# Self attention of a Perceiver layer: the value product and its way back move into the loop, the Ev product is turned in 32x32 blocks by VectorE, each batch enters the next stage by itself, two PSUM banks are kept across stages

## The chip, the cores and the metric

The kernel runs on one core of a Trainium2 chip, all in fp32. The metric is device time in microseconds (us). The core has five engines, each with a queue of its own that is worked off in order: TensorE (PE in the profile, its weight loads PEld), VectorE (DVE), ScalarE (ACT), GpSimd (POOL) and SyncE (SP), which here only starts transfers. TensorE writes to PSUM, eight banks of 128 partitions by 512 floats; the other engines bring results from there to SBUF. Engines wait for one another by semaphores.

## The reference

The shapes are x (4, 128, 512), ctx (4, 2048, 512), 16 heads of 32.

```python
x = x + xattn(layernorm(x), ctx, ctx)   # softmax over heads and batch (axis 0)
x = x + attn(layernorm(x))
x = x + ffn(layernorm(x))               # an attention too, with gates

def attn(x):        # rel[l,m] = clip(l - m, -64, 64) + 64
    q, k, v = heads(x @ Wq), heads(x @ Wk), heads(x @ Wv)
    logits = (q k^T + q . Ek[rel] + k . Eq[rel] + Eq[rel] . Ek[rel]) / sqrt(32)
    p = softmax(logits)                  # over m
    return p @ v + einsum('bhlm,lmd->bhld', p, Ev[rel])
```

The last term is the Ev product: for each row l there is another table Ev[rel[l, :]] of 128 by 32, common to the 64 pairs of head and batch.

## The kernel before, in words

Three stages follow each other: cross attention to about 661 us, self attention to 789.7, the gated attention ("ffn") to the end. The order of instructions in each engine's queue is the order in which the code issues them (`manual_schedule`); semaphores are put in between by the framework, for each use of a tile and for the reuse of a buffer. A pool with `bufs=n` holds n buffers, given out in turn; a new tile waits for the last reader of the one that it takes the place of.

Layouts: `x1` is [position, batch, 512]. `xT`, `qT`, `kT` and `oT` have features on the partitions: four chunks c of 128 features, four heads i in each, and columns (batch, position). `lg` and `eT` hold 64 tiles of 128x128, one for each f = (c, i, batch), in `lg` with rows l, in `eT` with rows m. "Group c" below means the four heads of chunk c, 16 tiles.

*The head of stage 2.* `layernorm_T` (L151) of stage 1 leaves x1 and xT, and at its end copies x out of PSUM (L224). `queries` and `keys` project; `spread` (L614) sorts q and k by position into `z`; `relative_k` and `relative_q` multiply them with the windows of Ek and Eq and lay the results into `rk` and `lg`. `ev_win`, the windows of Ev, then takes the place of `z`. PSUM: three banks `ps`, one `psz` (both opened for stage 2), and two pairs `ps4`, which `banks` takes together.

*The loop.* `logits(c)` transposes 16 tiles of rk into four banks (L717) and adds q k^T on top (L730). `join(c)` (L746, VectorE) adds the four banks to `lg`, `largest(c, i)` (L752, VectorE) takes the negated maximum, `exponentials_of(c, i)` (L757, ScalarE) are four instructions with a sum each, `softmax(c, i)` is a reciprocal on VectorE (L763) and a product on GpSimd (L764), `transposed(c, i)` four transposes (L772) and a copy to `eT` (L773; VectorE for heads 0 and 1, ScalarE for 2 and 3). A round issues `logits(c+1)`, all 16 exponentials of group c, all of join(c+1), and then, head by head, `largest(c+1, i)`, `softmax(c, i)` and `transposed(c-1, i)`:

```python
for c in range(C):
    if c + 1 < C:
        ps = logits(c + 1)
    for i in range(NH):
        exponentials_of(c, i)
    if c + 1 < C:
        join(c + 1, ps)
    for i in range(NH):
        if c + 1 < C:
            largest(c + 1, i)
        softmax(c, i)
        if c:
            transposed(c - 1, i)
```

*The end of stage 2.* Behind the loop, `attend(c)` puts the transposed x1 into a bank (L783), adds the products of v and eT for 16 pairs of head and batch (L795), and the sum goes to `oT` (L803). The Ev product (L848) multiplies, for each position p = 32 g + j, the window of Ev (128x32) with the 64 columns of `eT` at p; row group g of a bank gets the result. Each of four banks holds eight j. From there 32 VectorE adds (L863, 32 partitions each) and 32 ScalarE copies (L865) with two GpSimd adds (L869) bring it into `oT`; 16 transposes (L873) turn `oT` back to rows of x, in four banks. `layernorm_T` takes statistics of each batch there, normalises, transposes (L232) to xT, with `idle` matmuls (L149) between, and copies the banks to x1 (L224).

*Stage 3* opens with eight other banks, four `psl` and four `ps`. Five bias rows are loaded by GpSimd's queue (L897 to L901). For each batch `queries(b)` (L244, with an add on VectorE and a square on ScalarE), `lengths` and `normalised` follow; then keys, transposed queries, its own loop over groups, gates, and the output product. The weights of stage 3 are loaded by SP's queue (L47), each as soon as the buffer is free.

Of the kernel before, what the change touches and what calls it, by code (L numbers as in the profile page):

```python
# [16 lines left out]
def perceiver_layer(ctx: ExitStack, tc: tile.TileContext, a: dict, out: bass.AP):  # L17
# [32 lines left out]
    def load_const(name, shape, src, pool=const):  # L50
        t = pool.tile(shape, F32, tag=name, name=name)
        nc.gpsimd.dma_start(out=t, in_=src)
        return t

    def load_row(name, n, pool=const):
        return load_const(f"row_{name}", [P, n], a[name].partition_broadcast(P), pool)
# [195 lines left out]

    with s1:
# [5 lines left out]
        ps_g = s1.enter_context(tc.tile_pool(name="s1_ps", bufs=2, space=PSUM))  # L259
# [4 lines left out]

        def bank(n):
            return ps_g.tile([P, 512], F32, tag="ps", name=f"ps_{n}")
# [86 lines left out]
        def exponentials_of(n, c):  # L353
            nc.scalar.activation(sg[n, c], sg[n, c], AF.Exp, scale=SCALE)  # L354
# [229 lines left out]
    with ExitStack() as s2:  # L584
# [4 lines left out]
        ps1 = s2.enter_context(tc.tile_pool(name="s2_ps", bufs=3, space=PSUM))  # L589
        psz = s2.enter_context(tc.tile_pool(name="s2_psz", bufs=1, space=PSUM))  # L590
        ps4 = s2_loop.enter_context(tc.tile_pool(name="s2_ps4", bufs=2, space=PSUM))

        def bank(n):
            return ps1.tile([P, 512], F32, tag="ps", name=f"s2_{n}")

        def bank_z(n):
            return psz.tile([P, 512], F32, tag="psz", name=f"s2_{n}")
# [64 lines left out]
        def values(b, between=None):  # L662

            ps = bank(f"v{b}")
            for k in range(C):
                if between and k == C // 2:
                    between()
                nc.tensor.matmul(  # L668
                    ps, lhsT=xT[:, k, b * T : (b + 1) * T], rhs=awv[:, k, :], start=(k == 0), stop=(k == C - 1)
                )  # L670
            nc.scalar.copy(v[:, b, :], ps)

        def queries(c):
            ps = bank(f"q{c}") if c < 3 else bank_z("q3")
            project_T(ps, awq, xT, c)
            (nc.scalar.mul if c % 2 else nc.vector.tensor_scalar_mul)(qT[:, c, :], ps, SCALE)

        def keys(c):
            ps = bank(f"k{c}") if c < 3 else bank_z("k3")
            project_T(ps, awk, xT, c)  # L680
            (nc.scalar.copy if c % 2 else nc.vector.tensor_copy)(kT[:, c, :], ps)
# [61 lines left out]
        def join(c, ps):  # L743
            for i in range(NH):
                fs = of_head(c, i)
                nc.vector.tensor_tensor(  # L746
                    lg[:, fs, :], ps[i].rearrange("p (b m) -> p b m", b=B), lg[:, fs, :], ALU.add
                )
# [12 lines left out]
        def softmax(c, i):  # L761
            fs = of_head(c, i)
            nc.vector.reciprocal(rs[:, fs], rs[:, fs])  # L763
            nc.gpsimd.tensor_tensor(  # L764
                lg[:, fs, :], lg[:, fs, :], rs[:, fs].unsqueeze(2).to_broadcast([P, B, T]), ALU.mult
            )

        def transposed(c, i):
            ps = bank(f"t{c}_{i}")
            fs = of_head(c, i)  # L770
            for b in range(B):
                nc.tensor.transpose(ps[:, b * T : (b + 1) * T], lg[:, fs.start + b, :], ident)  # L772
            (nc.scalar.copy if i >= 2 else nc.vector.tensor_copy)(  # L773
                eT[:, fs, :], ps.rearrange("p (b l) -> p b l", b=B)
            )


        oT = one.tile([P, C, B, T], F32, tag="qT", name="oT2")

        def attend(c, eng):  # L780
            ps = bank_z(f"o{c}") if c % 2 else bank(f"o{c}")
            for b in range(B):
                nc.tensor.matmul(  # L783
                    ps[:, b * T : (b + 1) * T],
                    lhsT=x1[:, b, c * P : (c + 1) * P],
                    rhs=ident,
                    is_transpose=True,
                    start=(b == 0),
                    stop=False,
                    skip_group_check=True,  # L790
                )
            for b in range(B):
                for i in range(NH):
                    h = c * NH + i
                    nc.tensor.matmul(  # L795
                        ps[i * HD : (i + 1) * HD, b * T : (b + 1) * T],
                        lhsT=v[:, b, h * HD : (h + 1) * HD],
                        rhs=eT[:, h * B + b, :],
                        start=False,
                        stop=True,  # L800
                        skip_group_check=True,
                    )
            eng(oT[:, c].rearrange("p b l -> p (b l)"), ps)  # L803

        ps = logits(0)
        join(0, ps)
        for i in range(NH):
            largest(0, i)
        for c in range(C):
            if c + 1 < C:  # L810
                ps = logits(c + 1)
            for i in range(NH):
                exponentials_of(c, i)
            if c + 1 < C:
                join(c + 1, ps)
            for i in range(NH):
                if c + 1 < C:
                    largest(c + 1, i)
                softmax(c, i)
                if c:  # L820
                    transposed(c - 1, i)
        s2_loop.close()
        psq = s2.enter_context(tc.tile_pool(name="s2_psq", bufs=4, space=PSUM))

        def bank_q(n):
            return psq.tile([P, 512], F32, tag="psq", name=f"s2_{n}")


        nc.scalar.activation(small.tile([P, 1], F32, tag="rt", name="rt2"), eps, AF.Sqrt)
        attend(0, nc.vector.tensor_copy)  # L830
        attend(1, nc.vector.tensor_copy)
        for i in range(NH):
            transposed(C - 1, i)
            if i == 1:
                attend(2, nc.vector.tensor_copy)
# [4 lines left out]
        oev = one.tile([P, C * B, NG4, J8], F32, tag="kT", name="oev")  # L840
        by_8 = oT.rearrange("p c b (g n j) -> p (c b) g n j", g=NG4, j=J8)
        for n in range(NJ // J8):
            bk8 = bank_q(f"ev{n}")
            ps = bk8.rearrange("p (j f) -> p j f", f=NF)
            for j in range(J8):
                for g in range(NG4):
                    p = NJ * g + n * J8 + j
                    nc.tensor.matmul(  # L848
                        ps[g * HD : (g + 1) * HD, j, :],
                        lhsT=ev_win[:, T - 1 - p, :],  # L850
                        rhs=eT[:, :, p],
                        start=True,
                        stop=True,
                    )
            if n == 0:
                attend(C - 1, nc.vector.tensor_copy)
            for g in range(NG4):
                from_ = ps[g * HD : (g + 1) * HD].rearrange("p j (c i b) -> p i c b j", i=NH, b=B)
                for i in range(NH):
                    rows = slice(i * HD, (i + 1) * HD)  # L860
                    if n % 2:
                        to = oT[rows, :, :, g * NJ + n * J8 : g * NJ + (n + 1) * J8]
                        nc.vector.tensor_tensor(to, from_[:, i], to, ALU.add)  # L863
                    else:
                        nc.scalar.copy(  # L865
                            oev[rows].rearrange("p (c b) g j -> p c b g j", b=B)[:, :, :, g, :], from_[:, i]
                        )
            if n % 2 == 0:
                nc.gpsimd.tensor_tensor(by_8[:, :, :, n, :], by_8[:, :, :, n, :], oev, ALU.add)  # L869
        out_ps = [bank_q(f"out{b}") for b in range(B)]  # L870
        for b in range(B):
            for c in range(C):
                nc.tensor.transpose(out_ps[b][:, c * P : (c + 1) * P], oT[:, c, b, :], ident)  # L873
        idle_ps = bank_z("idle")[:, 0:P]
        xT = layernorm_T(out_ps, ps1, 2, keep=lambda k: idle(idle_ps, k))
# [9 lines left out]
    with ExitStack() as s3:  # L885
# [11 lines left out]
        fbq_row = load_row("ffn_bq", D, one)  # L897
        qe_row = load_row("ffn_query_embedding", D, one)
        fbv_row = load_row("ffn_bv", D, one)
        fbp_row = load_row("ffn_bp", D, one)  # L900
        brs_row = load_row("ffn_brs", H + 1, one)  # L901
# [17 lines left out]
        def queries(b):  # L919
            ps = bank_l(f"q{b}")  # L920
            project(ps, fwq, xT, b)
            nc.vector.tensor_tensor(q[:, b, :], ps, fbq_row, ALU.add)
# [99 lines left out]
        sqs = {0: queries(0)}  # L1022
        for b in range(B):
            lengths(b, sqs[b])
            if b + 1 < B:
                sqs[b + 1] = queries(b + 1)
            normalised(b)
# [178 lines left out]
```

## Time and profile before

| | us |
|---|---|
| runs | 874.06, 872.05, 871.6 |
| median of the runs | 872.05 |
| profiled execution | 871.75 |
| its span, first to last instruction | 869.8 |
| stage 1, to about | 661 |
| stage 2, head, to the first exponentials' inputs | 661 to 721.65 |
| stage 2, loop, to the start of the Ev product | 721.65 to 764.86 |
| Ev product | 764.86 to 775.98 |
| way back, to the first query product of stage 3 | 775.98 to 789.72 |
| stage 3, from there | 789.72 to 869.8 |

Over the span TensorE is busy 96%, VectorE 72%, ScalarE 50%, GpSimd 50%. From 661 to 721.65 TensorE is busy for 58.68 of 60.65 us; in the loop for 29.90 of 43.21, VectorE for 28.75, ScalarE for 31.66, GpSimd for 16.27; on the way back TensorE for 8.28 of 13.74, VectorE for 10.90.

How it is read: a timeline lists an engine's work in order of time: start, length, engine and line, operation, output and inputs, tile shape, count, and in brackets the idle time before it and what ended it. Neighbours of one line come as one row with a count. A window shows the busy time of each engine in a stretch (in the order TensorE, its weight loads, VectorE, ScalarE, GpSimd), then the clock that the throttle granted TensorE, as a share of full speed. In the page's row of 40 slices the same clock stands in tenths.

### The profile page before, as it was taken

To read this page: it belongs to the slowest core of one execution; us is meant where nothing else is said; L and a number is where in the kernel's file an instruction comes from. 1 tells how busy PE (TensorE), PEld (TensorE's weight loads), DVE (VectorE), ACT (ScalarE), POOL (GpSimd) and SP (SyncE) were. 2 spreads that over 40 slices of the span, in tenths; PEclk is the share of its full clock that TensorE was granted. 3 is DMA by queue.
4 is the path that set the end of the run, shared out by engine and by line. 5 is a ranking of instruction groups with operands and counts; after the bars stand their busy time and mean duration, and the time that the engine had idled before them with its cause. 6 is when DMAs were issued, how large, how long until landed. Compare 5 with 4: busy or idle time off the path is not lost. (4 is left out here: it accounts for less than half of the span.)

```text
span 869.8 us, 16501 instructions
## 1 busy us (share of the span) xinstructions
PE 831.1 (96%) x7109; PEld 450.1 (52%) x7109; DVE 625.6 (72%) x617; ACT 438.8 (50%) x730; POOL 437.9 (50%) x295
## 2 busy tenths in 40 slices
PE   9999999999999999999999999999989996779998
PEld 5454544554544545545554544544445565566564
DVE  2049688888888888988878888888963537556563
ACT  3358446465465455455464464554403555844671
POOL 1246766666757567666566757567700022512152
PEclk9999999999999999999999999999999999789999
DMA  8140010110101001010110101001101203002101
GB/s 301 34 142 2 1 49 2 49 50 1 50 1 49 11 39 50 1 50 1 50 49 2 49 2 49 2 1 50 48 2 49 96 4 146 2 2 50 50 2 49
DMA packets 10906, 35.55 MB, mean 41 GB/s; under 512 B 977, under 2 KB 1138, under 8 KB 8786
## 3 DMA queue, kind: packets, MB, share of 16 engines
q1 hardware_dynamic: 8402, 29.43, 9.5%
q10 hardware_dynamic: 1632, 3.15, 1.0%
q0 software_dynamic: 800, 1.93, 0.9%
q8 instruction: 56, 0.92, 0.4%
q14 instruction: 16, 0.13, 0.0%
HBM read 33.45 MB, written 1.05 MB: 40 GB/s over the span
## 5 line engine op out<-in xcount | busy, mean ns | idle before, releaser
L345 DVE TENSOR_TENSOR sg<-sg,stat 128x2048 f32<-128x2048 f32 x128 | 288.2, 2281 | 1.2
L354 ACT ACTIVATE sg<-sg 128x2048 f32<-128x2048 f32 x64 | 122.4, 1912 | 244.9 <-DVE sg L345 244.9
L244 PE MATMUL ps_v<-w_xattn_Wv,ct 128*128 128x512 f32 x512 | 232.6, 598 | 3.6 <-ACT v L291 3.3
L237 PE MATMUL ps_k<-ct,w_xattn_Wk 128*128 128x512 f32 x480 | 221.9, 605 | 0.8 <-ACT pos L142 0.8
L360 POOL TENSOR_TENSOR sm<-sm,sg 128x1024 f32<-128x1024 f32 x46 | 108.6, 2360 | 145.5 <-ACT sg L354 143.3
L324 DVE TENSOR_TENSOR mx<-mx,ps_s 128x1024 f32<-128x1024 f32 x96 | 117.2, 1221 | 78.1 <-ACT sg L315 65.9
L244 PEld LDWEIGHTS ps_v<-w_xattn_Wv,ct 128*128 128x128 f32 x512 | 96.3, 191 | 130.6 <-issue 113.9
L237 PEld LDWEIGHTS ps_k<-ct,w_xattn_Wk 128*128 128x128 f32 x480 | 86.2, 189 | 94.1 <-issue 86.1
L315 ACT COPY sg<-ps_s 128x1024 f32<-128x1024 f32 x128 | 124.2, 1020 | 7.2 <-DVE mx L322 3.5
L361 POOL TENSOR_TENSOR sm<-sm,sg 128x1024 f32<-128x1024 f32 x46 | 108.8, 2366 | 3.6
L292 POOL TENSOR_TENSOR v<-v,row_xattn_bv 128x512 f32<-128x512 f32 x64 | 81.7, 1277 | 41.4 <-ACT v L291 38.0
L302 PE MATMUL ps_s<-qT,kT 32*128 32x128 f32 x2048 | 75.7, 283 | 0.1
L389 PEld LDWEIGHTS pso<-sg,v 128*32 128x32 f32 x1920 | 49.2, 110 | 47.5 <-DVE mx L324 22.0
L302 PEld LDWEIGHTS ps_s<-qT,kT 32*128 32x128 f32 x2048 | 63.3, 186 | 18.0 <-issue 17.0
L389 PE MATMUL pso<-sg,v 128*32 128x128 f32 x1920 | 65.3, 277 | 3.7 <-DVE acc L402 2.1
L358 POOL TENSOR_TENSOR sm<-sg 128x1024 f32<-128x1024 f32 x16 | 37.9, 2366 | 45.3 <-ACT sg L354 45.2
L656 POOL TENSOR_TENSOR lg<-lg,pos 128x512 f32<-128x512 f32 x6 | 7.4, 1263 | 85.9 <-ACT lg L655 85.9
L285 ACT ACTIVATE kT<-ps_k,bk 128x512 f32<-128x512 f32 x64 | 44.2, 694 | 11.9 <-PE ps_k L237 6.0
L291 ACT COPY v<-ps_v 128x512 f32<-128x512 f32 x64 | 36.4, 569 | 10.1 <-PE ps_v L244 10.1
L402 DVE TENSOR_TENSOR acc<-pso,acc 128x512 f32<-128x512 f32 x54 | 36.9, 682 | 3.9 <-PE pso L389 3.9
L322 DVE TENSOR_TENSOR mx<-sg,ps_s 128x1024 f32<-128x1024 f32 x16 | 19.5, 1220 | 27.3 <-ACT sg L315 27.3
L995 POOL TENSOR_TENSOR e<-e,rs 128x512 f32<-128x512 f32 x16 | 16.3, 1041 | 40.6 <-DVE rs L994 40.6
(213 smaller groups left out, 834.7 us busy)
## 6 DMA issues: line engine op xcount, KB each, us to landing
ct<-in_ctxT SPq DMA_DIRECT2D x15, 1024.0 KB, 4.9
ev_win<-in_tabv SPq DMA_DIRECT2D x1, 2048.0 KB, 9.3
w_xattn_Wk<-in_xattn_Wk ACTq DMA_DIRECT2D x4, 256.0 KB, 7.9
ct<-in_ctxT SPq DMA_DIRECT2D x4, 256.0 KB, 6.5
x<-in_x SPq DMA_DIRECT2D x4, 256.0 KB, 8.0
w_xattn_Wv<-in_xattn_Wv ACTq DMA_DIRECT2D x1, 1024.0 KB
w_xattn_Wq<-in_xattn_Wq SPq DMA_DIRECT2D x1, 1024.0 KB, 10.4
w_xattn_Wo<-in_xattn_Wo ACTq DMA_DIRECT2D x1, 1024.0 KB, 5.3
```

Of the source, the lines that this page charges most:

```text
L237: nc.tensor.matmul(ps, lhsT=w[:, k, c * P : (c + 1) * P], rhs=src[:, k, :], start=(k == 0), stop=(k == C - 1))
L244: nc.tensor.matmul(ps, lhsT=src[:, k, b * T : (b + 1) * T], rhs=w[:, k, :], start=(k == 0), stop=(k == C - 1))
L285: nc.scalar.activation(kT[n, c], ps, AF.Identity, bias=bk[:, c : c + 1])
L292: nc.gpsimd.tensor_tensor(v[n, b], v[n, b], bv_row, ALU.add)
L302: nc.tensor.matmul(ps[i][:, cols], lhsT=kT[n, c][rows, cols], rhs=qT[rows, c, cols], start=True, stop=True)
L315: nc.scalar.copy(sg[n, c][:, k * HALF : (k + 1) * HALF], pss[n, c][k])
L324: nc.vector.tensor_tensor(mxs[n], mxs[n], pss[n, c][k], ALU.max)
L345: nc.vector.tensor_tensor(g, g, stat[:, row, :].unsqueeze(1).to_broadcast([P, NH * B, T]), op)
L354: nc.scalar.activation(sg[n, c], sg[n, c], AF.Exp, scale=SCALE)
L360: eng.tensor_tensor(t, t, g[:, 0:HALF], ALU.add)
L361: eng.tensor_tensor(t, t, g[:, HALF:], ALU.add)
L389: nc.tensor.matmul(ps[i * HD : (i + 1) * HD, b * T : (b + 1) * T], lhsT=v[n, b][:, h * HD : (h + 1) * HD], rhs=sg[n, c][:, f * T : (f + 1) ...
```

## The change

Stage 1 and the head of stage 2 keep their work; only their banks change. Two banks, `s12_ps`, live through both stages and serve the projections, `attend` and `turned_back`; two others, `s2_pst`, serve the transposes of the loop. After the loop the Ev product has one tile of four banks, `ev`.

In the loop, the exponentials of one head at a time alternate with the rest of the round. `join(0)` alternates with `largest(0, i)`, the table of the exponential is loaded before the loop, and `logits(c+2)` is issued at the end of round c. `attend(c-1)` has no x1 in it any more; its bank goes to `oT` by ScalarE (VectorE in the last round), and `turned_back` transposes `oT` and adds it to x1 on VectorE. All copies of eT of heads 2 and 3 stand inside the next group's round, between its heads 0 and 1.

Behind the loop, the Ev product goes on in one piece, with `attend(3)` after its fourth and `turned_back(3)` after its twelfth position, and 12 idle matmuls. For each batch `turn` transposes the 32x32 blocks of `ev` into `turned` in one VectorE instruction, an add (VectorE for batch 0, GpSimd for the others) brings it into x1, and statistics and the normalised `xn` of each batch follow by themselves (ScalarE). The transposes to xT move into stage 3, each batch's between the query products. The five rows go by SP's queue. The diff, cut to its core:

```diff
+    s12 = ctx.enter_context(ExitStack())
+    ps_g = s12.enter_context(tc.tile_pool(name="s12_ps", bufs=2, space=PSUM))
...
-        ps1 = s2.enter_context(tc.tile_pool(name="s2_ps", bufs=3, space=PSUM))
-        psz = s2.enter_context(tc.tile_pool(name="s2_psz", bufs=1, space=PSUM))
+        pst = s2.enter_context(tc.tile_pool(name="s2_pst", bufs=2, space=PSUM))
...
-        def join(c, ps):
-            for i in range(NH):
+        def join(c, ps, heads=range(NH)):
+            for i in heads:
...
-        def softmax(c, i):
+        def softmax(c, i, eng=nc.gpsimd):
...
-        def transposed(c, i):
-            ps = bank(f"t{c}_{i}")
+        def transposed(c, i, eng):
+            ps = bank_t(f"t{c}_{i}")
...
-        def attend(c, eng):
-            ps = bank_z(f"o{c}") if c % 2 else bank(f"o{c}")
-            for b in range(B):
-                nc.tensor.matmul(
-                    ps[:, b * T : (b + 1) * T],
-                    lhsT=x1[:, b, c * P : (c + 1) * P],
-                    rhs=ident,
-                    is_transpose=True,
...
+        def attend(c):
+            ps = bank(f"o{c}")
...
+        def attended(c, ps, eng):
+            eng(oT[:, c].rearrange("p b l -> p (b l)"), ps)
+
+        def turned_back(c):
+            ps = bank(f"ob{c}")
+            for b in range(B):
+                nc.tensor.transpose(ps[:, b * P : (b + 1) * P], oT[:, c, b, :], ident)
+            xc = x1[:, :, c * P : (c + 1) * P]
+            nc.vector.tensor_tensor(xc, ps.rearrange("p (b d) -> p b d", b=B), xc, ALU.add)
...
+        act, dve = nc.scalar.copy, nc.vector.tensor_copy
+        nc.scalar.activation(small.tile([P, 1], F32, tag="rt", name="rt4"), eps, AF.Exp)
+        ps = logits(0)
+        for i in range(NH):
+            join(0, ps, (i,))
+            largest(0, i)
+        ps = logits(1)
+        for c in range(C):
+            last = c + 1 == C
+            eng = dve if last else act
+            exponentials_of(c, 0)
+            if not last:
+                join(c + 1, ps)
+            softmax(c, 0)
+            if c:
+                transposed(c - 1, 2, eng)
+                transposed(c - 1, 3, eng)
+            if not last:
+                largest(c + 1, 0)
+            exponentials_of(c, 1)
+            softmax(c, 1)
+            transposed(c, 0, dve)
+            if not last:
+                largest(c + 1, 1)
+            if c:
+                attended(c - 1, attend(c - 1), eng)
+            exponentials_of(c, 2)
+            softmax(c, 2)
+            if c:
+                turned_back(c - 1)
+            if not last:
+                largest(c + 1, 2)
+            transposed(c, 1, dve)
+            exponentials_of(c, 3)
+            if c + 2 < C:
+                ps = logits(c + 2)
+            if not last:
+                largest(c + 1, 3)
+                softmax(c, 3)
...
+        transposed(C - 1, 2, dve)
+        softmax(C - 1, 3, nc.vector)
+        transposed(C - 1, 3, dve)
+        ev = psq.tile([P, NJ, NF], F32, tag="ev", name="ev")
+        for j in range(NJ):
+            if j == 4:
+                attended(C - 1, attend(C - 1), act)
+            if j == 12:
+                turned_back(C - 1)
...
+        idle(bank_t("idle")[:, 0:P], 12)
...
+        def turn(b):
+            nc.vector.transpose(
+                turned[:, b, :].rearrange("p (h d) -> p h d", d=HD),
+                ev.rearrange("p j (h b) -> p b h j", b=B)[:, b],
+            )
...
+        turn(0)
+        add(0, nc.vector)
+        statistics(0)
+        turn(1)
+        add(1, nc.gpsimd)
+        normalised(0)
+        turn(2)
+        add(2, nc.gpsimd)
+        statistics(1)
+        turn(3)
+        add(3, nc.gpsimd)
+        normalised(1)
+        statistics(2)
+        normalised(2)
+        statistics(3)
+        normalised(3)
...
-        fbq_row = load_row("ffn_bq", D, one)
...
+            load_row(name, n, one, nc.sync)
...
-        sqs = {0: queries(0)}
+        def x_turned(b):
+            ps = bank_l(f"xT{b}")
+            for c in range(C):
+                nc.tensor.transpose(ps[:, c * P : (c + 1) * P], xn[b][:, c * P : (c + 1) * P], ident)
+            nc.scalar.copy(xT[:, :, b * T : (b + 1) * T], ps.rearrange("p (c t) -> p c t", c=C))
+        x_turned(0)
+        ps = queries(0)
         for b in range(B):
-            lengths(b, sqs[b])
             if b + 1 < B:
-                sqs[b + 1] = queries(b + 1)
-            normalised(b)
+                x_turned(b + 1)
+            sq = queries_out(b, ps)
+            if b:
+                normalised(b - 1)
+            lengths(b, sq)
+            if b + 1 < B:
+                ps = queries(b + 1)
+        normalised(B - 1)
```

## Prediction

> **What bounds the kernel now.** I read the page first (span and granted clock), then the timeline of each engine from 655 to 805 us, the only stretch that the change reaches, then windows of 1 us there. Stage 1 issues the same instructions in the same order in both kernels, and so does stage 3 behind its query product.
>
> ```profile
> span 869.8 us, 16501 instructions
> ...
> PEclk9999999999999999999999999999999999789999
> ```
>
> The page: the clock is below full only in slices 35 and 36, the self attention. ScalarE and VectorE there (timeline; start, length, what ended the idle time before):
>
> ```profile
> 725.10 2.48 DVE L746 TENSOR_TENSOR lg<-s_l,lg 128x512 f32<-128x512 f32 x4 [2.40 <-PE s_l L730]
> 727.50 2.45 DVE L752 TENSOR_REDUCE nm<-lg 128x4 f32<-128x512 f32 x4
> ...
> 728.26 1.28 ACT L757 ACT_TABLE_LOAD   x1 [9.39 <-DVE nm L752]
> ...
> 743.72 0.59 ACT L773 COPY eT<-s_t 128x512 f32<-128x512 f32 x1 [1.27 <-PE s_t L772]
> ...
> 771.38 9.60 DVE L863 TENSOR_TENSOR oT<-s_ev,oT 32x128 f32<-32x128 f32 x32 [1.64 <-PE s_ev L848]
> ```
>
> From 729.55 to 758.4 ScalarE holds the path: 64 exponentials 0.383 apart are 24.5 us, and it idles only 1.27 and 0.81. It streams because its copies of eT stand behind all 16 exponentials of a group. TensorE after that:
>
> ```profile
> 742.60 1.09 PE L772 MATMUL s_t<-ident,lg 128*128 128x128 f32 x4 [5.61 <-ACT eT L773]
> 743.48 3.62 PE L717 MATMUL s_l<-ident,rk 128*128 128x128 f32 x16
> ...
> 764.86 2.52 PE L848 MATMUL s_ev<-eT,ev_win 128*32 128x64 f32 x64 [0.73 <-ACT eT L773]
> ...
> 781.12 3.65 PE L873 MATMUL s_out<-ident,oT 128*128 128x128 f32 x16 [5.15 <-DVE oT L863]
> ...
> 789.72 13.97 PE L244 MATMUL s_q<-w_ffn_WqT,xT 128*128 128x512 f32 x32 [0.32 <-DVE xT L232]
> ```
>
> The Ev product ends at 775.98; 13.74 us pass before the query product of stage 3, most of them L863. The query product ends at 803.53, and 66.3 us of work that stays as it is follow.
>
> **The change, part by part.** I lay the new instructions in their queues' order with these rows' durations: 0.61 per VectorE pass over 128x512 (0.68 to its end), 1.04 per POOL product (L764), 0.53 per four transposes (0.60 to their end), 3.36 per `logits`, 1.02 per `attend`, 0.05 to 0.1 per hand-over. First at full clock.
>
> *Two banks kept.* The first query product of stage 2 waited 1.19 for copies of x (L224); now only for the last xT copy (659.69+0.69): 1.07 gained. But k2 needs the bank of k0, whose eviction stands on VectorE behind ten z copies (6.10): 0.6 lost. `logits(0)` starts at 721.15, not 721.65.
>
> *Loop head.* The table load (1.28) moves ahead, into ScalarE's idle 9.39; `join` and `largest` alternate, so the first exponential waits for one join, not four (1.9). It starts at 726.0 instead of 729.55. The price: the fourth join ends at 729.2 instead of 727.6, and it frees the banks of the second half of `logits(1)`, which ends at 731.5. Then four joins to 734.0, one maximum to 734.6. ScalarE, done with group 0 at 732.2, idles 2.5.
>
> *The loop.* The change puts waiting instructions into queues that streamed. In group 1:
> - ScalarE has the copies of eT(0,2), eT(0,3) behind one head instead of four. They wait for transposes that stand on TensorE behind `logits(2)`, which stands behind t(0,0) and t(0,1). Those wait for POOL's softmax(0,0) and (0,1), whose reciprocals stand on VectorE behind join(1), at 734.0. So t(0,0) 735.1, t(0,1) 736.1 to 736.7, `logits(2)` to 740.0, t(0,2) at 740.5. Head (1,0) is done at 736.2: 4.4 idle. The other twelve exponentials of the group stand behind.
> - The copy of oT(0) stands before head (1,2). It waits for `attend(0)`, behind t(1,0), which waits for a reciprocal behind join(2) (742.5): POOL 743.6, t(1,0) 744.2, `attend` 745.3. ScalarE idles 2.2.
> - Group 2 repeats it: 0.60, 0.45 and 1.80.
>
> From 726.0: 24.5 of exponentials, six copies of about 0.5, idle 2.5+4.4+2.2+0.6+0.45+1.8 = 12.0 make 765.4, against 758.4. Before it was 24.5, two exposed copies each in groups 1 and 2, and 2.1 idle.
>
> *Loop end.* Three `attend` are done by now (before: L783 and L795 from 757.17 on). After the last exponential come a reciprocal, a product on VectorE (0.69), four transposes, a copy: Ev starts at 769.8, 4.4 later instead of 6.5 later. That is 4.9 behind the 764.86 of before. Ev with `attend(3)` and four transposes takes the same 11.1, since the transposes of x (L783) are gone: 780.9.
>
> *The way back.* Removed: 32 L863 (9.60), 32 copies L865 beside them, two POOL adds, 16 transposes (3.65 at half clock) and the x copies. Added on the path: one block turn, an add (0.69), statistics (0.72+0.18), a root (0.29), two small passes (0.3), xn (0.69), four transposes (0.6), a copy (0.59) and nine hand-overs. No row has a 32x32 turn. The nearest passes are VectorE's copy from PSUM (L773, 0.66) and L658, which reads PSUM at the same stride of 64 floats at 0.65: 0.69. The Trainium skill ("VectorE: DVE Perf Modes", The three transpose paths) has 311 ns for 128 columns of bf16. Four of those, an estimate, are 1.24. I take the row; four turns at 1.24 add about 1.1 in all. So 5.4 instead of 13.74: the query product starts at 786.3. Of each later batch, four transposes and a copy now lie between two query products: 0.55+0.74 twice, and once 1.7 because the copy stands behind the statistics of all batches. The product ends at 804.5, not 803.53.
>
> *Queues.* Five row loads go from POOL (0.54 each) to SP. Their space is ev_win's, so they go out when Ev ends: 781 and 3.8 to land; first use is 789.9. On SP they stand before the load of ffn_Wp, which waits for the last query product anyhow. POOL gets three adds of 1.27, of which turns and statistics cover all but 0.5. Without that cover each row would cost its landing time.
>
> Sum at full clock: about +1.0 at 804.5, some +0.7 at the end.
>
> **The clock.** It decides. Windows (PE busy, then PEld, DVE, ACT, POOL; the number before DMA share and GB/s is the granted clock):
>
> ```profile
> 741.00:742.00 1.00, 0.00 (x0) 0.00 (x0) 1.00 (x3) 1.00 (x7) 0.79 (x2) 0.50 0.00 0
> ...
> 754.00:755.00 1.00, 0.91 (x4) 0.52 (x4) 1.00 (x6) 1.00 (x7) 0.83 (x1) 0.63 0.00 0
> ...
> 782.00:783.00 1.00, 1.00 (x7) 1.00 (x6) 0.71 (x2) 0.00 (x0) 0.00 (x0) 0.50 0.06 16
> ...
> 785.00:786.00 1.00, 1.00 (x10) 1.00 (x10) 0.93 (x5) 0.99 (x3) 0.67 (x2) 1.00 0.00 0
> ```
>
> Half clock ran 740.6 to 747.4, 754.3 to 757.7 and 778.2 to 785.0: multiples of 3.41. The fall at 754.3 came with no gap over 1.25; TensorE was busy some 40% of the 3.4 us before (1.25, 1.04, 0.60 idle in the timeline). About 55% (723.6 to 727.0) kept the clock. The Trainium skill ("TensorE: Matmul & The Clock Gate", Why this matters for your kernels) warns of gaps over about 3 us. By it only the gap of 3.7 us before t(0,0) trips, and t(0,0), t(0,1) and part of `logits(2)` cost 2 more: +3, 875. By the rows also the stretches with gaps of 2.6 (before t(1,0)), 2.2, 1.7 and 1.9 (group 3), 1.7 (before t(3,3)) and 1.4 (before xT0) trip. Doubled on the path: first knot 2.0, t(1,0) and `attend(0)` 1.6, group 2 0.5, t(3,3) with `attend(3)` and early Ev 1.2, half of the first query product 1.7: 7.0. Where the 3.4 us grid falls decides which are hit, so I take 6, from 1 (the first knot in part) to 8.5. (The same page says in its Part 4 that transposes don't count as busy. Here transposes alone, 781.6 to 784.6, brought the clock back at 785.0.)
>
> Together +7. Profiled span 869.8+7 = 876.8; around the span lay 1.95 (871.75-869.8); the median of the runs is 0.3 above that execution: 872.05+7 = **879.0**.
>
> **Rivals.**
> - *The clock stays full.* For it: `idle` fills 2.7 us at the edge, and TensorE gets more work per group. Against it: the 3.7 us gap at the loop head. Only +0.7: 872.8, within 0.3%, which is about what a measurement here can tell.
> - *Faster.* One thing would do it: t(0,3) is done when head (1,0) ends at 736.2, so that no copy stops the exponentials. Then 4.4 idle in group 1 and 1.0 in group 2 go, the gaps on TensorE shrink with them, and the sum is +0.7-5.4 with about 2 of clock loss: 869. For it: before, t(0,2) ran at 736.33. Against it: `logits(2)` stands ahead of t(0,2) and needs join(1), done at 734.0. It decides from about 4 us less idle in the two groups.
> - *The turn is dear*, a quarter of the row's rate (2.4 us each, four on or near the path): 5 more, 884. Against it: L658 reads the same stride at full rate.
> - *Doing nothing* is excluded: exponentials and copies swap places on ScalarE whatever the durations.
>
> **How the numbers follow.** Throttled loop 0.68 (own range 875 to 883), dear turn 0.14 (880 to 885), full clock 0.10, faster 0.08. So slower 0.82, same 0.10, faster 0.08. Range 872.5 to 884: it takes in the full-clock case, leaves out the faster one and the top of the dear turn.
>
> **What would show it.** Idle on ScalarE before the eT copy in group 1 ended by PE, about 4 us or more, and before the oT copy about 2 to 4; last exponential at 765 or later; Ev starting 5 to 11 later than 764.86; under 7 us from Ev's end to the first query product; granted clock 0.5 in several stretches between 733 and 800. Wrong if exponentials run through group 1, if the clock stays at 1.0 there, or if a turn takes over 1.3 us.

## The result and the profile after

The changed kernel takes 880.67 us (median of 878.65, 878.7, 882.64 and 882.8) against 872.15: a ratio of 1.0106, interval 1.0085 to 1.0127, about 9 us slower. The prediction was 879.0, range 872.5 to 884. The four runs lie in two pairs 4 us apart; the profiled execution (882.8, span 880.9) is of the upper pair, so its trace shows about 2 us more than the median. The span and the clock on the page:

```profile
span 880.9 us, 16406 instructions
...
PEclk9999999999999999999999999999999998699999
```

The low slices are those of the self attention, as before. How much of it ran slow the 1-us windows tell: 30.7 us at half clock from the first logits to about the end of stage 3's query product, against 17.1. The timelines of the engines after the change, in the order in which the events cause each other (start, length, engine and line, ..., in brackets idle before and what ended it):

```profile
733.31 2.48 DVE L744 TENSOR_TENSOR lg<-s_l,lg 128x512 f32<-128x512 f32 x4 [3.22 <-PE s_l L728]
735.71 0.17 DVE L761 RECIPROCAL rs<-rs 128x4 f32<-128x4 f32 x1
736.02 2.04 POOL L762 TENSOR_TENSOR lg<-lg,rs 128x512 f32<-128x512 f32 x2 [16.84 <-DVE rs L761]
737.12 2.11 PE L770 MATMUL s_t<-ident,lg 128*128 128x128 f32 x8 [3.84 <-POOL lg L762]
739.02 2.39 PE L715 MATMUL s_l<-ident,rk 128*128 128x128 f32 x16
742.45 1.09 PE L770 MATMUL s_t<-ident,lg 128*128 128x128 f32 x8
743.14 1.07 ACT L771 COPY eT<-s_t 128x512 f32<-128x512 f32 x2 [5.00 <-PE s_t L770]
748.88 0.58 ACT L791 COPY oT<-ps_o 128x512 f32<-128x512 f32 x1 [3.13 <-PE ps_o L781]
756.08 1.07 ACT L771 COPY eT<-s_t 128x512 f32<-128x512 f32 x2 [1.98 <-PE s_t L770]
761.23 0.58 ACT L791 COPY oT<-ps_o 128x512 f32<-128x512 f32 x1 [2.54 <-PE ps_o L781]
776.79 1.35 PE L861 MATMUL ev<-eT,ev_win 128*32 128x64 f32 x32 [0.78 <-DVE eT L771]
...
788.76 0.72 DVE L874 STREAM_TRANSPOSE evT<-ev 128x512 f32<-128x512 f32 x1 [5.27 <-PE ev L861]
794.27 5.40 PE L244 MATMUL s_q<-w_ffn_WqT,xT 128*128 128x512 f32 x8 [0.73 <-ACT xT L1078]
799.51 0.60 PE L1077 MATMUL s_xT<-ident,xn 128*128 128x128 f32 x4
800.78 3.70 PE L244 MATMUL s_q<-w_ffn_WqT,xT 128*128 128x512 f32 x8 [0.68 <-ACT xT L1078]
```

The first seven lines are the knot of group 1. Four joins, then the reciprocal behind them, then GpSimd's product, then eight transposes, then `logits(2)` (L715 and L728), then the next eight transposes, and only then ScalarE's copies, in front of which ScalarE idled 5.00. The next three are the same wait at the later copies. The last five are the edge: Ev at 776.79, a block turn of 0.72, the query product at 794.27, and between two query products four transposes and a wait of 0.68 for their copy.

Stage by stage, from the traces of all profiled executions (read from the first logits on; the start of the logits itself varied by 2.8 us among them, on both sides of the change, so only differences of stages are compared; each row is one execution, with the half clock that it happened to have):

| | logits to Ev | Ev product | way back | query product | after it | half clock |
|---|---|---|---|---|---|---|
| before | 43.21 | 11.12 | 13.74 | 13.97 | 66.1 | 17.1 |
| after | 55.52 | 11.91 | 5.57 | 19.84 | 66.8 | 30.7 |
| end alone | 43.19 | 13.18 | 5.59 | 18.46 | 66.7 | 13.7 |
| loop alone | 58.37 | 11.15 | 14.43 | 13.97 | 66.1 | 41.0 |
| reciprocal first | 50.48 | 11.10 | 5.57 | 18.47 | 66.8 | 20.5 |
| kept warm | 50.73 | 11.09 | 5.57 | 19.76 | 66.7 | 10.2 |
| copies on VectorE | 55.62 | 11.91 | 5.56 | 19.84 | 66.8 | 34.1 |
| first join whole | 52.34 | 11.09 | 5.57 | 18.46 | 66.8 | 17.1 |
| order mended | 45.14 | 11.09 | 5.57 | 15.70 | 66.7 | 10.2 |
| order mended, kept warm | 43.56 | 11.09 | 5.57 | 15.80 | 66.7 | 0.0 |
| both best | 38.60 | 13.18 | 6.23 | 15.70 | 66.8 | 0.0 |
| both best, without idle matmuls | 40.89 | 13.18 | 5.57 | 17.38 | 66.7 | 13.7 |

After against before: -0.4 until the first logits, +12.3 in the loop, +0.8 in Ev, -8.2 on the way back, +5.9 in the query product, +0.7 behind it: 11.1, the difference of the spans.

### The profile page after: what moved, and what is told of

It is laid out like the page before. It is cut to its first block, busy times and chain, and to the rows that moved or that the text cites. A ratio compares the mean times of both kernels' runs of the same rounds, so it can differ in the third digit from the quotient of the medians.

```text
span 880.9 us, 16406 instructions
## 1 busy us (share of the span) xinstructions
PE 836.1 (95%) x7093; PEld 451.6 (51%) x7093; DVE 623.1 (71%) x595; ACT 430.3 (49%) x697; POOL 435.3 (49%) x290
## 3 DMA queue, kind: packets, MB, share of 16 engines
HBM read 33.45 MB, written 1.05 MB: 39 GB/s over the span
## 5 line engine op out<-in xcount | busy, mean ns | idle before, releaser
L1045 POOL TENSOR_TENSOR e<-e,rs 128x512 f32<-128x512 f32 x16 | 16.3, 1039 | 40.8 <-DVE rs L1044 40.8
## 6 DMA issues: line engine op xcount, KB each, us to landing
w_xattn_Wq<-in_xattn_Wq SPq DMA_DIRECT2D x1, 1024.0 KB, 10.2
```

## The experiments

**The end without the loop.** Edit, against the kernel before: its loop stays; `attend` loses x; behind the loop everything is the changed kernel's.

```diff
-        attend(0, nc.vector.tensor_copy)
-        attend(1, nc.vector.tensor_copy)
+        attended(0, attend(0), dve)
+        attended(1, attend(1), dve)
         for i in range(NH):
             transposed(C - 1, i)
             if i == 1:
-                attend(2, nc.vector.tensor_copy)
+                attended(2, attend(2), dve)
...
+            if j in (10, 12, 14, 16):
+                turned_back((j - 10) // 2)
```

> The loop of the kernel before, with the end of the changed one: value products behind the loop as before but without x in them, four transposes back and adds to x1 inside the Ev product, block turn, each batch by itself into stage 3, rows by SP's queue. Theory (the loop lost 12 us, the end gained 4): in the changed kernel the way from the end of the Ev product to the first query product took 5.6 us instead of 13.7, and from there to the end of the query product 19.7 (18.0 at full clock) instead of 13.8; so 4 us less than before, 868 (866 to 870), and half clock only in the loop's two old stretches. Rival (the end costs: the transposes between the query products give back what the turn gains): 872 or more.

Measured: 868.77, ratio 0.9967 (0.9951 to 0.9982), against 871.56 before: 2.8 faster. The way back is worth 8.15 (13.74 to 5.59) and the query product costs 4.5, as expected. The expectation named the four transposes back inside the Ev product but left their time out of its sum: 13.18 instead of 11.12. The rival, that the end costs, falls.

**The loop without the end.** Edit, against the changed kernel: `attend` with the transposes of x in it (as before), no `turned_back`, and behind the loop the 32 adds, 32 copies, 16 transposes and `layernorm_T` of the kernel before.

```diff
+                nc.tensor.matmul(
+                    ps[:, b * T : (b + 1) * T],
+                    lhsT=x1[:, b, c * P : (c + 1) * P],
...
-            if c:
-                turned_back(c - 1)
...
-            nc.vector.transpose(
...
+        xT = layernorm_T(out_ps, ps_g, 2, keep=lambda k: idle(idle_ps, k))
```

> Loop, banks and head of the changed kernel (attend with x in it again, no transposes back in the loop), end of the kernel before (32 adds, 32 copies, 16 transposes, four batches into xT, rows by GpSimd's queue). Theory: the Ev product starts about 12 later than in the kernel before, the end takes its old 13.7, so 882 to 885. Rival (the end is what costs): 875 or less, with the Ev product starting within 5 of before.

Measured: 885.06, ratio 1.0147 (1.0119 to 1.0175), 13.5 slower. Logits to Ev took 58.37. So the loop loses and the end gains; the two runs add up to +10.7, near the +8.5 of both together (in this run `attend` also carries the transposes of x, which the changed kernel has not).

**What holds the loop: the reciprocal moved.** One statement of the changed kernel, two lines up:

```diff
             exponentials_of(c, 0)
+            softmax(c, 0)
             if not last:
                 join(c + 1, ps)
-            softmax(c, 0)
```

> The changed kernel with one statement moved: softmax(c, 0), that is the reciprocal of the first head of a group on VectorE and its product on GpSimd, stands ahead of the four joins of the next group instead of behind them. Theory (the reciprocals stand on VectorE behind joins, GpSimd starts late, the transposes on TensorE start late, logits and joins of the next group stand behind those, and the copies on ScalarE wait for all of it): the first product on GpSimd starts at 732.4 instead of 736.0, the idle 5.0 of ScalarE before its first copies of eT shrinks by 2 or more in each group, and the time falls by 3 to 6, to 875 to 878. Rival (the gaps come from the copies being in ScalarE's queue, wherever the reciprocal stands, or from the clock alone): within 1.5 of 880.7.

Measured: 874.73, ratio 1.0041 (1.0028 to 1.0055): 6 less than the changed kernel from a move of 0.17 us of work. The timelines of ScalarE and GpSimd:

```profile
730.12 1.04 POOL L762 TENSOR_TENSOR lg<-lg,rs 128x512 f32<-128x512 f32 x1 [12.47 <-DVE rs L761]
736.55 1.04 POOL L762 TENSOR_TENSOR lg<-lg,rs 128x512 f32<-128x512 f32 x1 [5.40 <-DVE rs L761]
...
743.32 1.07 ACT L771 COPY eT<-s_t 128x512 f32<-128x512 f32 x2 [5.24 <-PE s_t L770]
745.83 0.57 ACT L791 COPY oT<-ps_o 128x512 f32<-128x512 f32 x1
751.45 0.59 ACT L771 COPY eT<-s_t 128x512 f32<-128x512 f32 x1 [0.42 <-PE s_t L770]
752.47 0.59 ACT L771 COPY eT<-s_t 128x512 f32<-128x512 f32 x1 [0.43 <-PE s_t L770]
754.50 0.59 ACT L791 COPY oT<-ps_o 128x512 f32<-128x512 f32 x1
```

The first product starts at 730.12 instead of 736.02. Before the copies of eT in group 1 nothing is won: the second product still starts at 736.55, because its reciprocal stands behind the joins, and the 5 us of idle stay; there the expectation missed. The other waits shrink or go: none before the copy of oT in group 1 instead of 3.13, and in group 2 0.42 and 0.43 before those of eT instead of 1.98, none before that of oT instead of 2.54. Half clock fell with it, from 30.7 to 20.5, so this one edit acts on queue and clock together. Runs with about the same granted clock over the span (0.983 to 0.987) part the two: seven of this kernel have a median of 874.2, two of the changed kernel lie at 878.7. Some 4.5 of the 6 stay.

**Copies taken from ScalarE.** Edit:

```diff
-            eng = dve if last else act
+            eng = dve
```

> The changed kernel with all the waiting copies taken out of ScalarE's queue: eT of heads 2 and 3 and oT are copied by VectorE in every round, at the same places in the order of issue. Theory after the run with the reciprocal moved (the chain reciprocal behind joins, product, transposes, logits, joins holds the loop, and the copies on ScalarE only show it): ScalarE's idle moves to before the exponentials, ended by VectorE's maximum, and the time stays within 1.5 of 880.7. The prediction's wording taken literally (waiting copies in the queue of the exponentials are what costs): the exponentials stream, the last ends 4 or more earlier than 771, and the time is 876 or less.

Measured: 882.99, ratio 1.0132 (1.0101 to 1.0164), no better than the changed kernel (1.0085 to 1.0127); it lies 2.3 above that kernel's median, where at most 1.5 was expected, and the other case, 876 or less, is out. ScalarE's timeline, the rows with a wait behind its first exponential:

```profile
736.84 0.40 ACT L755 ACTIVATE lg<-lg,nm 128x128 f32<-128x128 f32 x1 [4.19 <-DVE nm L750]
739.94 0.40 ACT L755 ACTIVATE lg<-lg,nm 128x128 f32<-128x128 f32 x1 [1.45 <-DVE nm L750]
747.28 0.40 ACT L755 ACTIVATE lg<-lg,nm 128x128 f32<-128x128 f32 x1 [2.61 <-DVE nm L750]
752.46 0.40 ACT L755 ACTIVATE lg<-lg,nm 128x128 f32<-128x128 f32 x1 [1.99 <-DVE nm L750]
760.28 0.40 ACT L755 ACTIVATE lg<-lg,nm 128x128 f32<-128x128 f32 x1 [4.63 <-DVE nm L750]
764.91 0.40 ACT L755 ACTIVATE lg<-lg,nm 128x128 f32<-128x128 f32 x1 [1.44 <-DVE nm L750]
```

With no copy in its queue ScalarE idles as much, 16.3 us against the 16.6 of the changed kernel's five waits (3.99 before the exponentials of group 1, then 5.00, 3.13, 1.98 and 2.54 before copies), now for maxima on VectorE. Its last exponential ends 3 us earlier (768.0), as six copies of 0.5 are gone, and Ev starts at 777.04 all the same. The joins start at 733.67, 742.91 and 755.91, in the changed kernel at 733.31, 742.55 and 755.49: the round through the engines takes as long. So the copies' place in ScalarE's queue does not make the wait. They stand in VectorE's queue here; a loop of this order without them was not run.

**The clock.** Edit: idle matmuls into the bank that is filled next, at the places where TensorE waits.

```diff
+        WARM = {(0, 0): 12, (1, 0): 8, (2, 0): 8, (2, 2): 5, (2, 3): 5, (3, 0): 3, (3, 3): 6, 0: 3, 1: 3, 2: 3}
...
         def transposed(c, i, eng):
             ps = bank_t(f"t{c}_{i}")
             fs = of_head(c, i)
+            idle(ps[:, 0:P], WARM.get((c, i), 0))
```

> The changed kernel with idle matmuls (0.245 us each at full clock in the idle row of the changed kernel) where TensorE waits in the loop: 12, 8, 8 and 3 ahead of the transposes of the first head of groups 0 to 3, 5 ahead of each of the last two heads of group 2, 6 ahead of the last transposes, 3 ahead of each transposes back of oT in the loop; they write to the bank that is filled next. Theory (6 of the 8.5 us are half clock, the rest is queues): granted clock mostly 1.0 from 733 to 777, time 4 to 6 less, 875 to 877, still above before. Rival (clock alone): 872 or less. Rival (queues alone, clock without effect): 880 or more, since idle matmuls can only delay.

Measured: 875.38, ratio 1.0043 (1.0026 to 1.0061), 5.3 less. Windows of this kernel (busy time of TensorE, its weight loads, VectorE, ScalarE, GpSimd; then the granted clock, DMA share, GB/s):

```profile
733.00:745.00 12.00, 10.46 (x129) 8.71 (x128) 8.98 (x21) 4.37 (x18) 6.18 (x6) 1.00 0.00 1
745.00:757.00 12.00, 11.19 (x139) 10.05 (x140) 7.37 (x16) 9.76 (x43) 4.16 (x4) 1.00 0.01 1
757.00:771.00 14.00, 11.84 (x143) 9.96 (x146) 8.99 (x19) 9.48 (x44) 5.16 (x5) 1.00 0.01 2
```

and of the changed kernel:

```profile
733.00:745.00 12.00, 6.70 (x72) 5.62 (x64) 8.89 (x19) 3.51 (x15) 4.11 (x4) 0.85 0.00 1
745.00:757.00 12.00, 9.48 (x100) 8.24 (x100) 6.28 (x15) 6.89 (x31) 4.12 (x4) 0.72 0.00 1
757.00:771.00 14.00, 8.84 (x88) 6.43 (x88) 7.94 (x18) 11.46 (x58) 6.15 (x6) 0.63 0.01 2
```

The clock stayed at 1.0 from 733 to the end of the loop; half clock was left ahead of it, from 724.8 to 731.6, and in the first query product, from 786.2 to 789.6. With 10.2 us of half clock, less than the 17.1 of the kernel before, the kernel is still 0.4% slower than that. So neither the clock alone nor the queues alone make the loss.

**The first join.** Edit:

```diff
+        join(0, ps)
         for i in range(NH):
-            join(0, ps, (i,))
             largest(0, i)
```

> The changed kernel with join(0) in one piece ahead of the four maxima of group 0, as before, instead of alternating with them. The prediction's sum (alternating starts the exponentials 1.9 earlier and costs 2.5 of idle behind group 0): about the same at full clock, 879.5 to 882. Theory after the first runs (the banks of the first logits come free 2.2 earlier, so the joins of group 1, the reciprocals behind them and the whole chain start 2 earlier, while ScalarE's late start costs nothing, since it waits for that chain anyhow): 2 to 4 less, 877 to 879.

Measured: 876.62, ratio 1.0058 (1.0033 to 1.0083): 4 less. TensorE's timeline of this kernel, and the same place in the changed one:

```profile
723.87 2.26 PE L715 MATMUL s_l<-ident,rk 128*128 128x128 f32 x16 [1.52 <-DVE lg L744]
726.06 1.17 PE L728 MATMUL s_l<-kT,qT 32*128 32x128 f32 x32
```

```profile
726.88 1.06 PE L715 MATMUL s_l<-ident,rk 128*128 128x128 f32 x8 [2.25 <-DVE lg L744]
729.52 1.74 PE L715 MATMUL s_l<-ident,rk 128*128 128x128 f32 x8 [1.57 <-DVE lg L744]
731.18 2.09 PE L728 MATMUL s_l<-kT,qT 32*128 32x128 f32 x32
```

Alternating gives the banks back in two halves, 2.6 apart, since a maximum stands behind each join, and already the first half lets TensorE start only 5.6 after the start of the first logits instead of 4.9. TensorE waits twice, 2.25 and 1.57, the clock falls at 729.8, and L728 takes 2.09 instead of 1.17. With the join whole, `logits(1)` runs in one piece at full clock, and the knot of group 1 starts at 727.26 instead of 733.31 (join(1) on VectorE in the two timelines; 3.8 of these 6.1 come from the edit, since the logits began 2.3 earlier in this execution). Four runs with a granted clock of 0.983 to 0.986 have a median of 877.0, against the 878.7 of the changed kernel's two at 0.984 and 0.987: more than half of the 4 goes with the clock.

**All of the change, in another order.** Edit: reciprocal first, first join whole, and in stage 3 the next batch's transposes in the middle of a query product:

```diff
+            for k in range(C):
+                if k == C // 2 and b + 1 < B:
+                    x_turned(b + 1)
+                nc.tensor.matmul(
+                    ps, lhsT=xT[:, k, b * T : (b + 1) * T], rhs=fwq[:, k, :], start=(k == 0), stop=(k == C - 1)
+                )
```

> The changed kernel with three things of its order mended: the first reciprocal of a group ahead of the joins, join(0) in one piece, and in stage 3 the transposes of the next batch in the middle of a batch's query product instead of behind it (their copy by ScalarE then lies beside the second half). All parts of the change are still there. Theory: 6 for the first (measured), 1 to 3 for the second, 2 for the third (three hand-overs of 0.7 at the query products go): 868 to 872, no slower than the kernel before. Rival (packing the value product into the loop costs by itself, since TensorE, VectorE and ScalarE get more work per group): 874 or more.

Measured: 867.33, ratio 0.9956 (0.9936 to 0.9976): 13 less than the changed kernel, 4.4 less than the kernel before, with value product, transposes back, block turn and two banks all still there. In TensorE's timeline the query products run without a wait behind the first:

```profile
783.28 1.99 PE L971 MATMUL s_q<-w_ffn_WqT,xT 128*128 128x512 f32 x4 [0.73 <-ACT xT L1083]
785.10 0.60 PE L1082 MATMUL s_xT<-ident,xn 128*128 128x128 f32 x4
785.54 3.60 PE L971 MATMUL s_q<-w_ffn_WqT,xT 128*128 128x512 f32 x8
788.98 0.60 PE L1082 MATMUL s_xT<-ident,xn 128*128 128x128 f32 x4
```

The product with its transposes takes 15.70, not 18.47 (full clock in both). The rival, 874 or more because packing the loop costs by itself, falls: most of the loss was the order. Not all of it: with the same end and the loop of the kernel before, the last experiment reaches 864.95, 2.4 less (without the two kept banks too), and its interval does not touch this one's. The same kernel with idle matmuls in the loop, and 15 instead of 12 behind the Ev product:

> The kernel with the order mended (all parts of the change in it, 867.3) with idle matmuls where TensorE waits in the loop (10, 4, 4 ahead of the first transposes of groups 0 to 2, 3 ahead of each of the last two heads of group 2, 6 ahead of the last, 3 ahead of one group's transposes back, 15 at the end). Theory: a little is left of the clock's part there (its profiled execution had 0.989 over the span): 0 to 3 less, 864 to 867. If they sit in front of work that is due: 868 or more.

Measured: 866.05, ratio 0.9927 (0.9907 to 0.9947), granted clock 1.0 over the span; the intervals overlap with those without.

**A version that beats both.** The loop of the kernel before, the end of the changed one, the transposes in the middle of the query products, the table of the exponential loaded before the first logits; with idle matmuls ahead of the first transposes of each group and 18 instead of 12 behind the Ev product, and without. Edit, against the kernel with the end alone, besides the diff above:

```diff
+        nc.scalar.activation(small.tile([P, 1], F32, tag="rt", name="rt4"), eps, AF.Exp)
         ps = logits(0)
         join(0, ps)
...
+        WARM = {(0, 0): 12, (1, 0): 8, (2, 0): 8, (3, 0): 4}
```

> Loop order of the kernel before, end of the changed one (as in the run with the end alone), with the table of the exponential loaded before the first logits (1.28 off the head), the transposes of the next batch in the middle of a query product (about 2), and idle matmuls ahead of the first transposes of each group (12, 8, 8, 4) and 18 instead of 12 at the end, against the half clock in the loop (up to 3). From 868.8: 863 to 866, faster than both kernels. If the idle matmuls only delay, 865 to 868.

> The fastest kernel so far (863.6) without its idle matmuls in the loop, and with 12 instead of 18 at the end. If these keep the clock and that is worth something: 865 to 868, with half clock in the loop again. If they do nothing: 863 to 864.

Measured: 863.59 with (0.9907, 0.9884 to 0.993), 864.95 without (0.9909, 0.9888 to 0.9929). Both are 0.9% faster than the kernel before. That the idle matmuls help is not shown by the times; from the logits on the trace has full clock and 38.60 to Ev with them, 13.7 us of half clock and 40.89 without.

## Why the prediction was right, and where it was off

The direction, the size (+7 for a measured +8.5) and the two causes, waits in the loop and the clock, held. The size is nearer than its terms. Taken by stages they add up to +7.6 (-0.5, +10.8, 0, -8.3, +5.9, -0.3), and the trace has +11.1. That the medians differ by 8.5 only is because the traced execution is of the upper pair; this part is luck.

*Loop.* The logits began 0.4 earlier, where 0.5 was said. From there to Ev 48.65 was worked out at full clock (721.15 to 769.8); 5.3 for the clock (2.0, 1.6, 0.5 and 1.2 of its list) makes 54.0; 55.52 came. The five waits on ScalarE were put at 2.5, 4.4, 2.2, 1.05 and 1.8 at full clock and came at 3.99, 5.00, 3.13, 1.98 and 2.54. The links of the chain were right, the reciprocals behind the joins among them. What was wrong is which link the text called the cause: "The change puts waiting instructions into queues that streamed", meant of ScalarE's copies. Moving those copies to another engine won nothing; moving one reciprocal gave 6.

*Loop head.* This is the step that failed. It had alternating `join` and `largest` as exponentials that start 1.9 earlier, at a price of 2.5 idle, at full clock. The early start won nothing, since ScalarE then idled 3.99 for the chain behind the late banks, and the run with the join whole is 4 faster. The list of stretches in which the clock would trip began with the first transposes; it fell already in `logits(1)`, after gaps of 2.25 and 1.57 that the step itself had made by giving back the banks in halves.

*Clock.* 6 was taken, from 1 to 8.5. Keeping the loop warm gave 5.3. In that run 2.1 more of the loop than worked out (50.73 against 48.65) go with the half clock left at 724.8 to 731.6, and 1.3 of the query product with that at 786.2 to 789.6; taken from its +3.8 this leaves about 0.4, where the sum at full clock had +0.7. This part is put together from stages, not measured. Of the six falls of the clock between 721 and 800 in the changed kernel one, at 736.6, lies in a gap of 3.84 on TensorE, two (746.8 and 760.5) follow gaps of 2.75, one (729.8) gaps of 2.25 and 1.57, and two (777.5 and 794.6) have no gap over 1.7 ahead of them. The last two are the gaps before t(3,3) and before the first xT, which the prediction had on its list from its rows. Those it had weighed against the Trainium skill ("TensorE: Matmul & The Clock Gate", Why this matters for your kernels: gaps over about 3 us), and the rows held. Only the share is off: the 3.4 us before the fall at 754.3, put at some 40% busy, have 1.55 of 3.41, or 45%.

*Way back and query product.* 5.4 and 18.2 at full clock were worked out; 5.57 and 18.46 to 18.47 came where the clock was full, 19.84 in the changed kernel, whose first product ran at half clock (5.40 for 3.70; the sum had 1.7 for it). The turn took 0.68 to 0.72, the row's 0.69 and not the 1.24 estimated from the Trainium skill ("VectorE: DVE Perf Modes", The three transpose paths). The rows on SP's queue delayed no work of stage 3: the first add that needs one followed the first query product.

*Behind the query product* +0.7 came where -0.3 was said without a reason; all kernels with the changed end have it (66.7 to 66.8), the loop alone with the old end has not (66.1). The traces place it. From the end of the last add on VectorE to the end of the span 3.22 pass before, 3.85 after, and 3.21 with the loop alone. There SyncE waits for the transfers' semaphores, one wait after another. That for the last output transfer is the fifth of nine in the kernel before and the second in the changed one, so the waits behind it take 0.28 before and 0.94 after. The five row loads added to SyncE's queue are the likely reason for the other place; no run moves them alone.

*The rivals.* Holding the clock in the loop gave 875.4, with 10.2 us of half clock left; 872.8 at full clock throughout was not tried. The faster case, in which no copy stops the exponentials, had been put at 869. The mended order is faster than that, 867.3, but it is another case: 2.8 of it come from the query product (18.47 to 15.70), and in group 1 ScalarE still idles 3.81 before the copies of eT.

## What to carry to other kernels

When work is packed into a loop of in-order queues, look for the ring of waits through all engines and ask at each link what stands ahead of it in its queue: here 0.17 us of reciprocal behind 2.5 us of joins cost 6 us, with the clock's part in it, while taking the waiting copies from the engine that showed the idle time won nothing. Where a producer waits for several banks, other work between the reads that free them holds it up: maxima put between four joins cost 4 us, the clock's part included. And part a change into its pieces before judging it: measured apart, this one held a gain of 3 and a loss of 13.

## What was not expected of the hardware

TensorE's clock fell to half in stretches of 3.41 us and their multiples (up to 10.2 in the changed kernel, from 760.5 to 770.7), and no long gap was needed. Windows of that length of the changed kernel, laid end to end so that the falls are on their bounds (busy time of TensorE first; the granted clock is the third number from the end):

```profile
722.93:726.35 3.42, 1.71 (x38) 1.34 (x36) 1.59 (x3) 0.12 (x1) 0.00 (x0) 1.00 0.91 383
726.35:729.76 3.41, 1.30 (x10) 1.13 (x11) 3.31 (x6) 3.41 (x19) 0.00 (x0) 1.00 0.35 149
729.76:733.17 3.41, 3.41 (x40) 2.89 (x38) 0.33 (x1) 2.74 (x15) 0.00 (x0) 0.50 0.02 5
...
770.72:774.13 3.41, 2.04 (x24) 1.28 (x12) 2.38 (x5) 1.83 (x4) 1.04 (x1) 1.00 0.00 0
774.13:777.54 3.41, 1.37 (x28) 1.17 (x32) 1.76 (x4) 0.00 (x0) 0.00 (x0) 1.00 0.00 0
777.54:780.95 3.41, 3.41 (x89) 3.25 (x82) 0.00 (x0) 0.61 (x1) 0.00 (x0) 0.50 0.02 5
```

TensorE was busy for 50% and 60% of the windows after which the clock stayed, and for 38% and 40% of those after which it fell. Laid out in the same way, the twelve traces have 342 windows at full clock between 690 and 812 us. After all 36 in which TensorE was busy for 48% or less the clock fell; of the 306 with 49% or more it fell after two (53% and 57%). The split was found in these traces and not tried on others. It fits that idle matmuls help: of 0.245 us each, they held the clock at 1.0 from 733 to 771, with TensorE busy for 33.5 of these 38 us (the three windows of that experiment) instead of 25.0.
